# Attention kernel over 200 gathered histories: two of four row tiles fetched by address return to the gathers, scaling and copying move from TensorE to ScalarE, and every gather states its bound

## The chip, the cores and the metric

The kernel runs on one core of a Trainium2 chip. The metric is the device time of one execution in microseconds. TensorE is PE in the profile, VectorE DVE, ScalarE ACT, GpSimd POOL and SyncE SP.

## The reference

A recommendation model scores 16,384 samples. Each has a user, an item, a category and 200 history items. For every history position l the rows of an embedding table (100,000 rows of 64 floats) are gathered, a small attention layer gives each sample a weight, and the weighted rows are summed:

```
h = i_emb[hist]                               # [200, 16384, 64]
feat = concat([h, it, h - it, h * it])
a = dice(feat @ au_W1 + au_b1, au_alpha, axis=1)   # moments over the 16384 samples
cur = sum(((a @ au_W2) + au_b2) * h, axis=0)
z = concat([u, it, c, cur])
z = dice(z @ W1 + b1, alpha1, axis=0)
z = dice(z @ W2 + b2, alpha2, axis=0)
return z @ W3 + b3
```

`dice(x)` is `x * (p + alpha * (1 - p))` with `p = sigmoid((x - mean) * rsqrt(var + eps))`. History indices lie from 0 to 99,999, category indices below 1000.

## The kernel before

The 16,384 samples are 128 tiles of 128. Eight columns c of 16 tiles each make up one history position l, so the work is 200 x 8 = 1,600 steps k = 8l + c. A step has a row buffer `rows` of 128 x 16 x 64 (one of five, `ROWS`), and the steps overlap: in step k the rows of k are fetched, those of k-1 are transposed and multiplied (`turn`, `product`), those of k-2 are read out of PSUM and measured (`hidden`, `measure`), and those of k-10 (`LAG`) are weighted and added to the sum (`gate`, `weights`, `weigh`). After eight columns `moments` makes mean and variance of the position. The order on each engine is written out by hand in `step` (L368 to L392). Forty-five positions make up one pass of a loop (`LPB`); the loop runs four passes and the last 20 positions stand after it.

**Three ways bring rows in.** The usual one is `gather` (L124 to L130): one indirect transfer on POOL reads 128 indices from a column of `idx` and fetches 128 rows. It states no bound. Of the 128 tiles of a position 124 go this way (`NC`, L74), 16 in an even column and 15 in an odd one. The last tile of columns 1 and 5 goes through SP (`rows_by_sync`): SP loads addresses into registers 16 at a time and issues one transfer per row, 32 rows in each step (`ask`, L398). The last tile of columns 3 and 7 goes through ScalarE (`rows_by_scalar`): eight addresses at a time, 32 rows in each step at two places in its order (L379, L384), with three semaphores `landed` of its own and a wait ahead of the use (`await_rows_by_scalar`). `turn` copies such a tile, on ScalarE, from `side` or `aside` into the row buffer (L339).

**Two works stand on TensorE rather than on ScalarE.** `ph` is a copy of the transposed rows `hT` in PSUM, made by a product with the unit matrix (L341). The weight of a sample is `alpha * x + (1 - alpha) * p * x`, summed over the hidden units with `au_W2`; it is made as two products into `wb`, one of `xs` with `blk_x` and one of `y = pg * xs` with `blk_p` (L316).

The whole begins with 128 gathers of the items, and ends with 256 gathers of categories and users and the head (the two dense layers and the output).

Of the kernel before, what the change touches and what calls it, by code (L numbers as in the profile page):

```python
# [9 lines left out]
I32 = mybir.dt.int32  # L10
AF = mybir.ActivationFunctionType
ALU = mybir.AluOpType
PSUM = bass.MemoryType.PSUM

P = 128
D = 64
EPS = 1e-8
CH = 512
S = 32
# [3 lines left out]
LAG = 10  # L23
XR = 9
IDX = 3
BY_SP = (1, 5)
BY_ACT = (3, 7)
SIDES = (1, 3, 5, 7)
LOAD = 16
GROUP = 8  # L30
ROW = 4 * D
U8 = mybir.dt.uint8

# [2 lines left out]
def din_kernel(  # L36
# [32 lines left out]
    ZA = P // 2  # L69
    ZB = Z1 - ZA  # L70
    NS = len(SIDES)
    NB, NA = len(BY_SP), len(BY_ACT)
    serial = iter(range(10**6))
    NC = NT - NS  # L74
    BODY = L - L % LPB if L > LPB else 0
    STATS = nc.vector.BN_STATS_DIM
# [5 lines left out]
    def make(name, *shape, dt=F32):  # L82
        return const.tile(list(shape), dt, name=name)
# [4 lines left out]
    def quarter(e, g, n=S):  # L88
        return slice((2 * e + g) * S, (2 * e + g) * S + n)
# [23 lines left out]
    idx = [make(f"idx{i}", P, NC, dt=I32) for i in range(IDX)]  # L113
    ids = [make(f"ids{i}", P, NT, dt=I32) for i in range(3)]
    side = [make(f"side{i}", P, D) for i in range(3)]
    aside = [make(f"aside{i}", P, D) for i in range(3)]
    landed = [tc.alloc_semaphore(f"landed{i}") for i in range(3)]
    addrs = make("addrs", 2 * S + 1, NS * P, dt=I32)
    addr = [addrs[i * S : i * S + 1] for i in range(3)]
    stats = [make(f"st{i}", P, 2 * ND, STATS) for i in range(3)]  # L120
    rstds = [make(f"rs{i}", P, 1) for i in range(3)]
    shifts = [make(f"sh{i}", P, 1) for i in range(3)]
# [1 line left out]
    def gather(dst, ids, n, table):  # L124
        nc.gpsimd.indirect_dma_start(  # L125
            out=dst[:, n, :],
            out_offset=None,
            in_=table,
            in_offset=bass.IndirectOffsetOnAxis(ap=ids, axis=0),
        )  # L130

    def load_ids(t, v):
# [23 lines left out]
    def layer(dst, pairs, first=True, last=True):  # L156
        for i in range(2):
            for j, (lhsT, rhs) in enumerate(pairs):
                nc.tensor.matmul(  # L159
                    dst[:, ts(i, CH)], lhsT, rhs[:, ts(i, CH)],  # L160
                    start=(first and j == 0), stop=(last and j == len(pairs) - 1),
                    skip_group_check=not (first and last),
                )
# [9 lines left out]
    blk_h = make("blk_h", P, P)  # L173
    blk_i = make("blk_i", P, P)
    blk_m = make("blk_m", P, P)
    blk_p = make("blk_p", P, P)
    blk_x = make("blk_x", P, P)
    unit = make("unit", P, P)
    au_w = make("au_w", P, 4, A)
    au_bias = make("au_bias", P, 1)  # L180
    au_al = make("au_al", P, 1)
# [4 lines left out]

    def attention_weights():
        nc.vector.memset(eps, EPS)
        for t in (blk_h, blk_i, blk_m, blk_p, au_bias, au_al, au_w2):
            nc.vector.memset(t, 0.0)  # L190
        nc.sync.dma_start(au_bias2, au_b2.partition_broadcast(P))
        for e in range(2):
            w = au_W1.rearrange("(g d) a -> d g a", d=D)[e * S : (e + 1) * S]
            for g in range(2):
                r = quarter(e, g)
                nc.sync.dma_start(au_w[r], w)
                for q, (a0, n) in enumerate(halves):
                    c, a = quarter(q, g, n), slice(a0, a0 + n)
                    nc.vector.tensor_add(blk_h[r, c], au_w[r, 0, a], au_w[r, 2, a])
                    nc.vector.tensor_sub(blk_i[r, c], au_w[r, 1, a], au_w[r, 2, a])  # L200
                    nc.vector.tensor_copy(blk_m[r, c], au_w[r, 3, a])
                    nc.vector.memset(blk_p[r, quarter(q, g)], 1.0)
        for g in range(2):
            for q, (a0, n) in enumerate(halves):
                r, a = quarter(q, g, n), slice(a0, a0 + n)
                nc.sync.dma_start(au_bias[r], col(au_b1)[a])
                nc.sync.dma_start(au_al[r], col(au_alpha)[a])
                nc.sync.dma_start(au_w2[r], au_W2[a])
        nc.vector.tensor_scalar(au_1al, au_al, -1.0, 1.0, ALU.mult, ALU.add)
        nc.vector.tensor_mul(au_1al, au_1al, au_w2)  # L210
        nc.vector.tensor_mul(au_al, au_al, au_w2)
        nc.vector.tensor_scalar_mul(blk_x, blk_p, au_al)
        nc.vector.tensor_scalar_mul(blk_p, blk_p, au_1al)
        nc.vector.tensor_copy(unit, lanes)
        nc.vector.tensor_single_scalar(unit, unit, float(P), ALU.is_equal)


    w1a = make("w1a", P, 4, P)
# [10 lines left out]
    al1a, al1b, al12 = make("al1a", P, 1), make("al1b", P, 1), make("al12", P, 1)  # L229
    same_a = make("same_a", P, P)  # L230
    same_b = make("same_b", P, P)
    lanes, lane = (ucT[i][:, :P].bitcast(I32) for i in range(2))

    def head_weights():
        for t in (w1a, w1b, w2a, w2b, w3, bias2, al2):
# [28 lines left out]

    flat = i_emb.rearrange("v d -> (v d)").bitcast(U8)

    def addresses(l, s, p0, n, engine):
        _, at = nc.values_load_multi_w_load_instructions(
            addr[l % 3][:, s * P + p0 : s * P + p0 + n],
            engines=(engine,), min_val=0, max_val=ROW * (V - 1),  # L270
            skip_runtime_bounds_check_because="the DMA checks the address against the table",
        )
        return [flat[ds(a, ROW)].rearrange("(o d) -> o d", o=1) for a in at]

    def rows_by_sync(m, part, n):
        l, j = divmod(m, NB)
        s, dst = SIDES.index(BY_SP[j]), side[m % 3].bitcast(U8)
        for p0 in range(part * n, part * n + n, LOAD):
            for j, row in enumerate(addresses(l, s, p0, LOAD, mybir.EngineType.SP)):
                nc.sync.dma_start(dst[p0 + j : p0 + j + 1], row)  # L280


    keys = {}

    def rows_by_scalar(m, part):
        l, j = divmod(m, NA)
        s, dst = SIDES.index(BY_ACT[j]), aside[m % 3].bitcast(U8)
        key = keys.setdefault(m, f"rows{next(serial)}")
        for j, row in enumerate(addresses(l, s, part * GROUP, GROUP, mybir.EngineType.Activation)):
            p = part * GROUP + j  # L290
            dma = nc.scalar.dma_start(dst[p : p + 1], row).then_inc(landed[m % 3], 16)  # L291
            tc.no_tile_sem_insts.add(dma.ins.name)
            tc.add_to_no_dep_group(key, dma.ins)

    def await_rows_by_scalar(m):
        if m in keys:
            fence = nc.scalar.wait_ge(landed[m % 3], 16 * P)
            tc.declare_fence(fence.ins, group=keys.pop(m))
            nc.scalar.sem_clear(landed[m % 3])

    def has_side(k):
        return k % ND in SIDES
# [7 lines left out]
    def gate(k):  # L310
        i = k // ND % 3
        nc.scalar.activation(pg, xs[k % XR], AF.Sigmoid, bias=shifts[i], scale=rstds[i])  # L312

    def weights(k):
        nc.vector.tensor_mul(y, pg, xs[k % XR])  # L315
        layer(wb, [(blk_x, xs[k % XR]), (blk_p, y)])  # L316

    def weigh(k):
        nc.vector.scalar_tensor_tensor(wb, wb, au_bias2, hT[k % LAG], ALU.add, ALU.mult)  # L319
# [10 lines left out]
    def turn(k):  # L330
        if has_side(k):
            l, c = divmod(k, ND)
            if c in BY_ACT:
                m = l * NA + BY_ACT.index(c)
                await_rows_by_scalar(m)
                of = aside[m % 3]
            else:
                of = side[(l * NB + BY_SP.index(c)) % 3]
            nc.scalar.copy(rows[k % ROWS][:, TD - 1], of)  # L339
        transpose(hT[k % LAG], rows[k % ROWS])  # L340
        layer(ph, [(unit, hT[k % LAG])])  # L341
        layer(px, [(blk_h, hT[k % LAG]), (blk_i, itT[k % ND])], last=False)

    def product(k):
        nc.vector.tensor_mul(hm, ph, itT[k % ND])  # L345
# [22 lines left out]
    def step(k, last=None):  # L368

        def has(j):  # L370
            return last is None or j <= last

        if has(k):
            fetch(k)
        if has(k - LAG):
            gate(k - LAG)
            weights(k - LAG)
        if has(k):
            scalar_rows(k, 0)  # L379
        if has(k - 2):  # L380
            hidden(k - 2)
            measure(k - 2)
        if has(k):
            scalar_rows(k, 1)  # L384
        if has(k - 1):
            turn(k - 1)
        if has(k - LAG):
            weigh(k - LAG)
        if has(k - 1):
            product(k - 1)  # L390
        if has(k - 2) and (k - 2) % ND == ND - 1:
            moments((k - 2) // ND)  # L392

    AHEAD = ND // NB - 1 - BY_SP[0]

    def ask(k, end):  # L398
        m, part = divmod(k + 1 + AHEAD, ND // NB)
        if m < end * NB:  # L400
            rows_by_sync(m, part, P * NB // ND)

    def scalar_rows(k, slot):
        m, part = divmod(k, ND // NA)
        n = P * NA // ND // GROUP
        for i in range(n)[slot::2]:
            rows_by_scalar(m, part * n + i)

    def steps(l0, n, end):
        for k in range(n * ND):  # L410
# [10 lines left out]
    with tc.manual_schedule():  # L421
# [4 lines left out]
        load_ids(ids[2], r_user)  # L426
        nc.gpsimd.iota(lanes, pattern=[[1, P]], base=P, channel_multiplier=-1)
        attention_weights()
        for t in (*hT, *xs, *side, *aside, hm):
            nc.vector.memset(t, 0.0)  # L430
        for t in curT:
            nc.vector.memset(t, 0.0)
# [14 lines left out]
            if c:  # L447
                transpose(itT[c - 1], rows[(c - 1) % ROWS])
        nc.vector.memset(rows[-1 % ROWS], 0.0)
        for k in range(-1 - AHEAD, 0):  # L450
            ask(k, L)
        head_weights()

    if BODY:
        with tc.For_i(0, BODY, LPB) as l0:  # L455
            with tc.manual_schedule():
                steps(l0, LPB, LPB + 1)
                await_rows_by_scalar(LPB * NA - 1)

    K = (L - BODY) * ND  # L460
    za = [hT[(K - LAG + c) % LAG] for c in range(ND)]
# [140 lines left out]
```

## Time and profile before

| | us |
|---|---|
| median of three runs (31616.96 to 31647.4) | 31644.94 |
| the profiled execution | 31616.96 |
| its span, first instruction to last | 31615.1 |
| first gather of the history starts at | 162.8 |
| first gather of the head starts at | 31159.5 |
| last gather of the head starts at | 31477.8 |
| median of a gather on POOL | 0.944 |
| median from a gather's issue to landing | 2.4 |

The profile is of one execution. A group's row names line, engine, operation, output and inputs, count, then busy time and the mean of one in ns, then the idle time of the engine just before these instructions and what ended most of it. "Issue" means that the engine waited for nothing that the profile shows. A row of the timeline has start, duration, engine, line, operation and, in brackets, the idle time before it and its releaser. A row of waits has the waiting engine and line, the releaser, the total in us, the number of waits and the longest. A row with three durations separated by slashes has minimum, median and maximum in ns.

### The profile page before, as it was taken

The page shows a single profiled execution, that of the slowest core. Times are in us where ns is not written, and L with a number is a line of the kernel's source. Part 1 is how long each engine was busy: PE and PEld are TensorE (multiplying, and loading weights), DVE is VectorE, ACT ScalarE, POOL GpSimd, SP SyncE. Part 2 cuts the span into 40 slices and gives each one's busy share as a digit, 9 for nine tenths or more (in the row PEclk, how much of TensorE's full clock was granted, in tenths as well). Part 3 has the DMA queues.
Part 4 walks back from the last instruction along what each step waited for, and adds up shares of the span by engine and source line. Part 5 has one row for each costly group of instructions (what it writes and reads, how often), then busy time and mean ns, then how long its engine had stood idle before and what let it go on. Part 6 is the DMA issues. An engine that isn't in the chain of part 4 may idle for free. (4 is left out here: it accounts for less than half of the span.)

```text
span 31615.1 us, 357535 instructions
## 1 busy us (share of the span) xinstructions
PE 20448.2 (65%) x38864; PEld 8357.2 (26%) x38864; DVE 15015.4 (47%) x18963; ACT 4479.6 (14%) x4670; POOL 23766.1 (75%) x25189
## 2 busy tenths in 40 slices
PE   5666666666666666666666666666666666666666
PEld 2222222222222222222222222222222222222222
DVE  4444444444444444444444444444444444444443
ACT  1111111111111111111111111111111111111111
POOL 7777777777777777777777777777777777777776
PEclk7888888888888888888888888888888888888887
DMA  1111111111111111111111111111111111111111
GB/s 29 28 28 28 28 28 28 28 28 28 28 28 28 28 28 28 28 28 28 28 28 28 28 28 28 28 28 28 28 28 28 28 28 28 28 28 28 28 28 23
DMA packets 1050292, 890.26 MB, mean 28 GB/s; under 512 B 644640, under 2 KB 644640, under 8 KB 1047784
## 3 DMA queue, kind: packets, MB, share of 16 engines
q0 software_dynamic: 805888, 826.84, 11.8%
q1 hardware_dynamic: 138920, 27.05, 0.4%
q10 hardware_dynamic: 102976, 13.32, 0.3%
q14 instruction: 2202, 18.04, 0.2%
q8 instruction: 306, 5.01, 0.1%
HBM read 865.03 MB, written 0.13 MB: 27 GB/s over the span
## 5 line engine op out<-in xcount | busy, mean ns | idle before, releaser
L125 POOL DMA_INDIRECT rows<-in_L_rec_i_emb,idx x24800 | 23403.2, 944 | 7593.5 <-issue 7032.1
L159 PE MATMUL ph<-hT,unit 128*128 128x512 f32 x6404 | 5658.4, 1029 | 10498.9 <-DVE hT L154 10498.9
L154 DVE STREAM_TRANSPOSE hT<-rows 64x512 f32<-64x512 f32 x6404 | 4518.8, 706 | 8256.8 <-DMA rows<-in_L_rec_i_emb,idx 4150.3
L328 DVE BATCH_NORM_STATS2 st<-xs 128x6 f32<-128x512 f32 x3204 | 2060.4, 685 | 7172.9 <-ACT xs L323 7172.9
L159 PEld LDWEIGHTS ph<-hT,unit 128*128 128x128 f32 x6404 | 1688.5, 295 | 13506.4 <-DVE hT L154 13334.4
L159 PE MATMUL px<-hT,blk_h 128*128 128x512 f32 x6404 | 3936.6, 702 | 0.0
L323 ACT ACTIVATE xs<-px,au_bias 128x1024 f32<-128x1024 f32 x1602 | 1784.3, 1114 | 14626.1 <-PE px L159 12323.9
L159 PE MATMUL wb<-y,blk_p 128*128 128x512 f32 x6440 | 3329.8, 599 | 455.3 <-DVE y L315 455.3
L159 PE MATMUL px<-itT,blk_i 128*128 128x512 f32 x6404 | 3368.8, 608 | 0.0
L159 PE MATMUL wb<-xs,blk_x 128*128 128x512 f32 x6440 | 3307.3, 595 | 51.5 <-PEq L455 39.9
L159 PE MATMUL px<-hm,blk_m 128*128 128x512 f32 x6408 | 3013.0, 592 | 40.5 <-DVE hm L430 40.5
L312 ACT ACTIVATE pg<-xs,sh,rs 128x1024 f32<-128x1024 f32 x1610 | 1939.8, 1205 | 3751.2 <-issue 2579.9
L315 DVE TENSOR_TENSOR y<-pg,xs 128x1024 f32<-128x1024 f32 x1610 | 1956.6, 1215 | 512.9 <-ACT pg L312 508.6
L159 PEld LDWEIGHTS px<-hT,blk_h 128*128 128x128 f32 x6404 | 1566.7, 245 | 2295.1 <-issue 2294.6
L319 DVE SCALAR_TENSOR_TENSOR wb<-wb,au_bias,hT 128x1024 f32<-128x1024 f32 x1610 | 2080.5, 1292 | 88.2 <-PE wb L159 36.0
L320 DVE TENSOR_TENSOR curT<-wb,curT 128x1024 f32<-128x1024 f32 x1610 | 1970.8, 1224 | 54.8
L345 DVE TENSOR_TENSOR hm<-ph,itT 128x1024 f32<-128x1024 f32 x1601 | 1941.2, 1212 | 0.0
L159 PEld LDWEIGHTS px<-itT,blk_i 128*128 128x128 f32 x6404 | 1374.9, 215 | 1925.3 <-issue 1925.3
L159 PEld LDWEIGHTS wb<-y,blk_p 128*128 128x128 f32 x6440 | 1212.0, 191 | 2081.7 <-issue 1445.9
L159 PEld LDWEIGHTS wb<-xs,blk_x 128*128 128x128 f32 x6440 | 1228.3, 191 | 1603.9 <-issue 1597.9
L159 PEld LDWEIGHTS px<-hm,blk_m 128*128 128x128 f32 x6408 | 1218.1, 190 | 1573.0 <-issue 1424.7
L339 ACT COPY rows<-aside 128x64 f32<-128x64 f32 x401 | 97.9, 244 | 2659.6 <-DMA aside<-in_L_rec_i_emb 2525.7
(155 smaller groups left out, 2171.5 us busy)
## 6 DMA issues: line engine op xcount, KB each, us to landing
aside<-in_L_rec_i_emb ACTq DMA_DIRECT2D x51200, 0.2 KB
side<-in_L_rec_i_emb SPq DMA_DIRECT2D x51200, 0.2 KB
rows<-in_L_rec_i_emb,idx POOLq DMA_INDIRECT x24800, 2.4
idx<-in_r_hist SPq DMA_DIRECT2D x200, 62.0 KB
addrs<-in_r_hist SPq DMA_DIRECT2D x200, 2.0 KB
rows<-in_L_rec_i_emb,ids POOLq DMA_INDIRECT x128, 2.4
rows<-in_L_rec_c_emb,ids POOLq DMA_INDIRECT x128, 2.4
rows<-in_L_rec_u_emb,ids POOLq DMA_INDIRECT x128, 2.4
```

What stands on the lines that cost most here:

```text
L125: nc.gpsimd.indirect_dma_start(out=dst[:, n, :], out_offset=None, in_=table, in_offset=bass.IndirectOffsetOnAxis(ap=ids, axis=0),)
L154: nc.vector.transpose(by_tile(dst[ts(e, D)], i), of[ts(i, D), :, ts(e, S)])
L159: nc.tensor.matmul(dst[:, ts(i, CH)], lhsT, rhs[:, ts(i, CH)], start=(first and j == 0), stop=(last and j == len(pairs) - 1), skip_group_c ...
L312: nc.scalar.activation(pg, xs[k % XR], AF.Sigmoid, bias=shifts[i], scale=rstds[i])
L315: nc.vector.tensor_mul(y, pg, xs[k % XR])
L319: nc.vector.scalar_tensor_tensor(wb, wb, au_bias2, hT[k % LAG], ALU.add, ALU.mult)
L320: nc.vector.tensor_add(curT[k % ND], wb, curT[k % ND])
L323: nc.scalar.activation(xs[k % XR], px, AF.Identity, bias=au_bias)
L328: nc.vector.bn_stats(stats[l % 3][:, 2 * c + i, :], xs[k % XR][:, ts(i, CH)])
L339: nc.scalar.copy(rows[k % ROWS][:, TD - 1], of)
L345: nc.vector.tensor_mul(hm, ph, itT[k % ND])
```

## The change

Of the four tiles fetched by address two remain, both through SP: the last tiles of columns 3 and 7 (`SIDES = (3, 7)`). `NC` becomes 126. ScalarE issues no rows any more, and its semaphores and `aside` go. ScalarE does two works that TensorE did: it copies `hT` into `ph`, and it applies `au_al` and `au_1al` to `pg` in a second pass, so that one product with `blk_w` (the 0 and 1 blocks) is left of the two into `wb`. Every gather gets `bounds_check`, the last row of its table, and `oob_is_err=False`: an index beyond it is skipped, and no error is reported. In the built program this gives each gather a register operand for the bound and a register move in front of it on POOL.

```diff
-BY_SP = (1, 5)
-BY_ACT = (3, 7)
-SIDES = (1, 3, 5, 7)
+SIDES = (3, 7)
...
             in_offset=bass.IndirectOffsetOnAxis(ap=ids, axis=0),
+            bounds_check=table.shape[0] - 1,
+            oob_is_err=False,
         )
...
-    def rows_by_scalar(m, part):
-        l, j = divmod(m, NA)
-        s, dst = SIDES.index(BY_ACT[j]), aside[m % 3].bitcast(U8)
-        key = keys.setdefault(m, f"rows{next(serial)}")
-        for j, row in enumerate(addresses(l, s, part * GROUP, GROUP, mybir.EngineType.Activation)):
-            p = part * GROUP + j
-            dma = nc.scalar.dma_start(dst[p : p + 1], row).then_inc(landed[m % 3], 16)
...
+    def rows_by_address(m, l, part, n):
+        s, dst = m % NS, side[m % 3].bitcast(U8)
+        for b in range(0, n, LOAD):
+            p0 = part * n + b
+            _, at = nc.values_load_multi_w_load_instructions(
+                addr[l % 3][:, s * P + p0 : s * P + p0 + LOAD],
+                engines=(mybir.EngineType.SP,), min_val=0, max_val=ROW * (V - 1),
+                skip_runtime_bounds_check_because="the DMA checks the address against the table",
+            )
+            for j, a in enumerate(at):
+                p = p0 + j
+                nc.sync.dma_start(dst[p : p + 1], flat[ds(a, ROW)].rearrange("(o d) -> o d", o=1))
...
         nc.scalar.activation(pg, xs[k % XR], AF.Sigmoid, bias=shifts[i], scale=rstds[i])
+        nc.scalar.activation(pg, pg, AF.Identity, bias=au_al, scale=au_1al)
...
         nc.vector.tensor_mul(y, pg, xs[k % XR])
-        layer(wb, [(blk_x, xs[k % XR]), (blk_p, y)])
+        layer(wb, [(blk_w, y)])
...
         transpose(hT[k % LAG], rows[k % ROWS])
-        layer(ph, [(unit, hT[k % LAG])])
         layer(px, [(blk_h, hT[k % LAG]), (blk_i, itT[k % ND])], last=False)
+        nc.scalar.copy(ph, hT[k % LAG])
...
-        if has(k):
-            scalar_rows(k, 0)
...
-        if has(k):
-            scalar_rows(k, 1)
...
-    AHEAD = ND // NB - 1 - BY_SP[0]
+    PER = ND // NS
 
     def ask(k, end):
-        m, part = divmod(k + 1 + AHEAD, ND // NB)
-        if m < end * NB:
-            rows_by_sync(m, part, P * NB // ND)
+        m, part = divmod(k + 1, PER)
+        if m < end * NS:
+            rows_by_address(m, m // NS, part, P // PER)
```

## The prediction

> **What bounds the kernel now.** I read the busy times first, then the groups, then POOL's own timeline, then who waits for whom.
>
> ```profile
> PE 20448.2 (65%) x38864; PEld 8357.2 (26%) x38864; DVE 15015.4 (47%) x18963; ACT 4479.6 (14%) x4670; POOL 23766.1 (75%) x25189
> POOL 7777777777777777777777777777777777777776
> ```
>
> POOL is the busiest at 75%, evenly over all slices; a share of 75% alone does not say that it is the bound. The group of its gathers does:
>
> ```profile
> L125 POOL DMA_INDIRECT rows<-in_L_rec_i_emb,idx x24800 | 23403.2, 944 | 7593.5 <-issue 7032.1
> ```
>
> Busy and idle together, 23403.2 + 7593.5 = 30,996.7 us, are nearly the span, and nearly all idle time is "issue": it waits for nothing. The timeline of POOL in mid-run and at a loop edge:
>
> ```profile
> 15000.58 0.94 POOL L125 DMA_INDIRECT rows<-in_L_rec_i_emb,idx  x1 [0.30 <-issue]
> 15001.83 0.94 POOL L125 DMA_INDIRECT rows<-in_L_rec_i_emb,idx  x1 [0.30 <-issue]
> 15003.08 0.94 POOL L125 DMA_INDIRECT rows<-in_L_rec_i_emb,idx  x1 [0.30 <-issue]
> ...
> 7129.46 0.94 POOL L125 DMA_INDIRECT rows<-in_L_rec_i_emb,idx  x1 [0.30 <-issue]
> 7139.70 0.94 POOL L125 DMA_INDIRECT rows<-in_L_rec_i_emb,idx  x1 [9.30 <-issue]
> ```
>
> A gather starts every 1.25 us: 0.94 of work and a fixed 0.30 between two. The only breaks are four loop edges with idle times of 9.30, 7.51, 7.51 and 2.96 us, 26.1 us over the usual 0.30. So the pitch is (30,996.7 - 26.1) / 24,800 = **1.2488 us**. Everyone else waits for it:
>
> ```profile
> PEld ph L159 <- DVE hT L154: 13334.4, 3201, 17.2
> ...
> DVE hT L154 <- DMA rows<-in_L_rec_i_emb,idx: 4150.3, 753, 7.8
> DVE hT L154 <- ACT rows L339: 3143.2, 579, 6.5
> ```
>
> TensorE waits for the transposes, and these for gathered rows (or for ScalarE's copy of a tile fetched by address). The kernel's time is a count of gathers times a pitch.
>
> **The change part by part.**
>
> *Two tiles go back to POOL.* NC goes from 124 to 126 gathers per l. Over 200 l that is 400 more, with no cover, on the engine that sets the end: 400 x 1.2488 = **+499.5 us**. The 128 gathers of the items and 256 of the head stay, so the changed kernel has 25,200 + 384 = 25,584.
>
> *ScalarE's address work goes.* Its 51,200 transfers, register moves and waits leave (16 rows took 6.27 us in the timeline, so 51,200 some 20,000 us of its queue), and with them q10's 0.3% of the DMA engines. None of this holds a gather back, so it gives nothing. What is late next is what was late before: the gather.
>
> *SP's rows keep their count and lead.* It issued columns 1 and 5 and now issues 3 and 7, again 51,200. A tile's last part is asked two steps before its copy in both (before: step 8l for step 8l+2; after: 8l+2 for 8l+4). A step becomes 15.75 gathers, 19.7 us, against 19.4. Nothing.
>
> *TensorE gives work to ScalarE.* The `unit` products into `ph` (5658.4 us) and the `blk_x` half of the weights (3307.3 us) go. ScalarE gets a 128x1024 copy into `ph` per step, like the L323 row (1114 ns), and a second pass over `pg`, like L312 (1205 ns). Per step it then has 1.2 + 1.2 + 1.1 + 1.1 us and copies and table loads, about 5.2 of 19.7. The copy waits for the transposes, and behind it in the queue stands the next step's gate; `y` on VectorE waits for that. The chain from landing on (copy 0.24, transposes 2.9, `ph` 1.1, `hm` 1.2, two products 1.9, `xs` 1.1) is 8.4 us, gate, second pass and `y` 3.6 more: within a step, and the five row buffers give more. Costed at nothing; the cover is 19.7 us of gathers, and a chain past that would cost its excess 1,600 times.
>
> *The register move.* In the built program every gather gets a register move (the bound) in front of it on POOL's queue, 25,584 of them. SP's row shows one:
>
> ```profile
> L280 SPq MOVE side<-in_L_rec_i_emb x51200: 29/29/38, 52.6 to 31022.5; - x200
> ```
>
> With the gap after it, it delays SP's next issue by 59 ns. On POOL there is cover: I set the records of its 537 semaphore waits in the first loop pass against their place in the program. 393 ran 7 gathers ahead of the running one, 104 ran 6 and 37 ran 8 ahead, and a gather during which one ran has the same median pitch, 1249 ns. The queue is far ahead of the worker, so 59 ns vanish; without that cover they cost 25,584 x 0.059 = 1,509 us.
>
> *The check itself* is what no row shows: the worker compares 128 indices with a bound and would leave some out (none here: the drawn indices are all inside the tables). The nearest rows on POOL are:
>
> ```profile
> L588 POOL MEMSET const-uint8-127<- 128x1 uint8 x1 | 0.1, 116 | 0.0
> L588 POOL MEMSET const-float32-0.0<- 128x1 f32 x1 | 0.1, 99 | 0.3 <-issue 0.3
> ```
>
> One instruction over one value per partition, the shape of an index column, takes 99 to 116 ns with everything around it. Upper end: a whole pass, +0.116 x 25,584 = +2,968 us. A gain is not excluded, since the error path goes; but with no index out of range that can save little more than a scalar step, nearest the 29 ns move. Lower end: -0.029 x 25,584 = -742 us. I take **zero**, the row it is nearest to being the gather itself, 128 rows in 944 ns whatever the table (i_emb, c_emb and u_emb all 944): a compare in a loop that already reads, scales and writes out each index should vanish.
>
> A rule speaks against the change. The gather spends 944 / 128 = 7.4 ns per row. The Trainium skill's "GPSIMD Engine Reference", section 3.1, says that data-dependent branching costs about 12 cycles an element on these cores, whose clock section 1 gives as 1.2 GHz. If the skip were such a branch it would cost, as an estimate from that page, 10 ns x 128 = 1.28 us a gather, and the sum would be near 64.9 ms. The row shows a loop cheaper per row than one such branch; no run here shows the skip yet.
>
> **The sum.** Span 31,615.1 + 499.5 = 32,114.6; the profiled execution took 31,616.96, 1.9 more: 32,116.5. That execution was the lowest of three, whose median is 31,644.94; from the median it is 32,144.4. I take 32,130, +1.5%.
>
> **Rivals.**
>
> *A, forecast: the bound is free.* 32,130, own range 31,900 to 32,400 (a pitch of -8 to +10 ns). For: the wait records, and the equal 944. Chance 0.45.
>
> *B, the check costs worker time.* Halfway to the upper end, 0.058 x 25,584 = +1,484, about 33,600; at the end 35,085. For: the gather of before carries no bound at all in the built program, so work is added, and every nanosecond of it is paid 25,584 times. Against: the 0.30 us between gathers could take in a little. Chance 0.28.
>
> *C, the other side: leaving out the error report shortens the gather.* It decides from the point where the two extra gathers are paid: 499.5 / 25,584 = 19.5 ns a gather. At 29 ns: 32,116 - 742 = 31,374, faster by 0.8%. For: no other engine needs more than SP's 32 rows at 0.39 us, 12.5 of a step's 19.7 us, so every nanosecond would count. Against: nothing is reported in either kernel. Chance 0.19.
>
> *D, the register operand ends the run-ahead.* Were each move held until the gather before it had read its register, 59 ns show: 32,116 + 1,509 = 33,625. For: the operand is read from a register that the next move writes again. Against: the waits, which also stand between gathers, held nothing back. Chance 0.06.
>
> *E, no bound reaches the worker.* Against: the built program has the register as an operand of every gather. The time is A's. Chance 0.02.
>
> **How the numbers follow.** About 0.2% is what a measurement can tell from no change, a pitch window of 5 ns here: it takes 0.03 from C and B together. Faster 0.18, within 0.2% 0.03, slower 0.79. The range runs from C's price to B's end, 31,370 to 35,085; beyond lie the deeper half of C and a per-index branch, some 0.16.
>
> **What would show it.** Right: 25,200 body gathers at 944 ns with 0.30 between; POOL idle on issue; ScalarE near 8.2 ms busy, TensorE near 11.5 ms. B: the mean of L117's group above 944 with the gap unchanged. D: gap near 0.36 with 944 unchanged. C: the mean below 925. Wrong altogether: POOL idle on a releaser other than issue for more than a few hundred us, above all on VectorE through the row buffers (ScalarE's copy into `ph` too late).

## The result, and the profile after

The changed kernel took **33,488 us** (median of four runs, 33,485.28 to 33,488.41) against 31,645.5 before: a ratio of 1.058, with a 95% interval of 1.057 to 1.060. The forecast was 32,130, and the rival that came true is B, the check that costs worker time (about 33,600). The profiled execution has a span of 33,486.4, 1,871.3 more than that of before.

POOL's busy share is nearly the same (76% against 75%), and so is its idle time for each gather. The busy times and the gathers' group:

```profile
PE 15624.0 (47%) x26020; PEld 6240.6 (19%) x26020; DVE 14943.1 (45%) x18956; ACT 7826.6 (23%) x7481; POOL 25517.3 (76%) x25589
...
L117 POOL DMA_INDIRECT rows<-in_L_rec_i_emb,idx x25200 | 25133.8, 997 | 7713.3 <-issue 7139.6
```

The count is 25,200, as forecast, but the mean of one is 997 ns where it was 944. Idle before is 7713.3 / 25,200 = 306 ns, as before. In the timeline the starts are 1.30 us apart instead of 1.25, and all of the difference is in the busy part:

```profile
15001.07 1.00 POOL L117 DMA_INDIRECT rows<-in_L_rec_i_emb,idx  x1 [0.30 <-issue]
15002.38 1.00 POOL L117 DMA_INDIRECT rows<-in_L_rec_i_emb,idx  x1 [0.31 <-issue]
15003.68 1.00 POOL L117 DMA_INDIRECT rows<-in_L_rec_i_emb,idx  x1 [0.30 <-issue]
```

Nobody else became the bound. In the list of waits POOL waits for "issue", and VectorE for gathered rows, now three times as long as before. The 3,143.2 us in which it waited for ScalarE's copy of fetched tiles have no row any more:

```profile
DVE hT L148 <- DMA rows<-in_L_rec_i_emb,idx: 12714.8, 1498, 10.2
POOL rows L117 <- issue: 7250.3, 23693, 8.1
```

The register moves are in the trace, on POOL's queue, one for each gather:

```profile
L117 POOLq MOVE  x25584: 29/29/39, 0.8 to 33339.7; - x200
```

They ran seven or eight gathers ahead of the running one in 25,194 of 25,584 cases. During 22,067 of the 25,584 gathers no move ran, and these took 997.4 ns in the mean, the other 3,517 took 997.2, so the moves are hidden. The sum in measured terms: 400 gathers x 1.2488 = 499.5 us, and 25,584 x (997.4 - 943.7) ns = 1,374 us, together 1,873 of the 1,871 measured.

In the runs of experiments 1 to 12 many instructions on SP's queue, and on ScalarE's where it issues rows, took 700 ns where the profile of before has 29 and 228 on SP's, and the kernel before took 49,000 us on these chips, so that of those runs only the gathers' durations are read; the cause was not found, and on one of the same chips it was gone later.

### The profile page after: what moved, and what is told of

It is laid out like the page before. It is cut to its first block, busy times and chain, and to the rows that moved or that the text cites. A ratio compares the mean times of both kernels' runs of the same rounds, so it can differ in the third digit from the quotient of the medians.

```text
span 33486.4 us, 250048 instructions
## 1 busy us (share of the span) xinstructions
PE 15624.0 (47%) x26020; PEld 6240.6 (19%) x26020; DVE 14943.1 (45%) x18956; ACT 7826.6 (23%) x7481; POOL 25517.3 (76%) x25589
## 3 DMA queue, kind: packets, MB, share of 16 engines
q0 software_dynamic: 818688, 839.97, 11.3%
## 5 line engine op out<-in xcount | busy, mean ns | idle before, releaser
L117 POOL DMA_INDIRECT rows<-in_L_rec_i_emb,idx x25200 | 25133.8, 997 | 7713.3 <-issue 7139.6
L153 PE MATMUL px<-hT,blk_h 128*128 128x512 f32 x6404 | 5631.5, 978 | 16412.0 <-DVE hT L148 16412.0
L306 ACT COPY ph<-hT 128x1024 f32<-128x1024 f32 x1601 | 1627.7, 1017 | 20119.3 <-DVE hT L148 20119.3
L153 PEld LDWEIGHTS px<-hT,blk_h 128*128 128x128 f32 x6404 | 1816.1, 314 | 19421.0 <-issue 18597.0
L153 PE MATMUL px<-itT,blk_i 128*128 128x512 f32 x6404 | 4715.2, 829 | 0.0
L153 PE MATMUL wb<-y,blk_w 128*128 128x512 f32 x6440 | 3417.2, 657 | 1285.9 <-DVE y L284 1270.4
L153 PEld LDWEIGHTS px<-itT,blk_i 128*128 128x128 f32 x6404 | 1851.6, 289 | 2836.5 <-issue 2836.5
L281 ACT ACTIVATE pg<-pg,au_al,au_1al 128x1024 f32<-128x1024 f32 x1610 | 1896.1, 1178 | 54.0
L153 PEld LDWEIGHTS wb<-y,blk_w 128*128 128x128 f32 x6440 | 1309.1, 207 | 3019.1 <-issue 1542.3
```

What stands on the lines that cost most here:

```text
L117: nc.gpsimd.indirect_dma_start(out=dst[:, n, :], out_offset=None, in_=table, in_offset=bass.IndirectOffsetOnAxis(ap=ids, axis=0), bounds_c ...
L153: nc.tensor.matmul(dst[:, ts(i, CH)], lhsT, rhs[:, ts(i, CH)], start=(first and j == 0), stop=(last and j == len(pairs) - 1), skip_group_c ...
L281: nc.scalar.activation(pg, pg, AF.Identity, bias=au_al, scale=au_1al)
L306: nc.scalar.copy(ph, hT[k % LAG])
```

## The experiments

The theory: stating a bound makes POOL's worker compare the indices, which takes some 53 ns of every gather and reaches the time in full. The rivals: that skipping takes the time and not the comparison (2); that ScalarE's new work or the two tiles do (3); that the register move does (4).

### 1, 5, 11 and 13: the change without its bound

```diff
             in_offset=bass.IndirectOffsetOnAxis(ap=ids, axis=0),
-            bounds_check=table.shape[0] - 1,
-            oob_is_err=False,
         )
```

This kernel was run four times; its time is read from the last run.

> The changed kernel without the two arguments of the gather; all else as changed (two tiles by address, ScalarE's copy and second pass). Theory 1 (the bound check takes time in POOL's worker, 53 ns a gather): gathers back at 944 ns, pitch 1.249 us, span 31,615 + 400 x 1.2488 = 32,115 us, time 32,115 to 32,145. Theory 2 (the skip mode, not the comparison, takes it): the same here. Rival 3 (the bound is free, and the gather is slowed by ScalarE's new work, the lower clock of TensorE or the 126-column index tile): gathers stay at 997 ns, time 33,490.

> The kernel of the first experiment once more, since the transfers by address of SP and ScalarE, not the gathers, set the time of all four runs of that call (register moves of 700 ns on both queues, where the profile of before has 29). Theory 1 (a stated bound costs 50 to 70 ns a gather, nothing else in the change does): where SP's moves take 29 ns, 944 ns a gather and 32,115 to 32,145 us. Rival 3 (ScalarE's new work or the two tiles cost more than their 400 gathers): 944 ns a gather, but a time above 32,200. Where the moves take 700 ns, again a time of some 47,000 that tells nothing of this.

> The kernel of the first experiment, for a chip on which SP's register moves take 29 ns as in the profile of before. Theory 1: 32,115 to 32,145 us. Rival 3 (ScalarE's new work or the two tiles cost more than their 400 gathers): above 32,200. Where the moves take 700 ns again: some 47,000.

> The changed kernel without the bound. Where the kernel before takes 31,620 us: by theory 1 32,115 to 32,145 us, 944 ns a gather. By rival 3 (ScalarE's copy and second pass delay the row buffers) above 32,200, with POOL waiting for transposes.

Measured: gathers of 943.9, 946.3, 946.3 and 945.5 ns, so that runs of one kernel differ by up to 2.4 ns. In the last run the time was 32,156 us against 31,674 of the kernel before on that chip, a ratio of 1.0152 (1.0135 to 1.0169). POOL's group there:

```profile
L117 POOL DMA_INDIRECT rows<-in_L_rec_i_emb,idx x25200 | 23825.5, 945 | 7709.1 <-issue 7267.6 <-DMA rows<-in_L_rec_i_emb,idx 417.0 <-DMA side<-in_L_rec_i_emb 21.4
```

So without the bound the change costs 482 us, where the 400 gathers alone were put at 499.5. Rival 3 falls: ScalarE's copy and second pass, the lower clock of TensorE and the wider index tile cost nothing. This is the forecast's case A, and its 1.5% was right for it.

### 2 and 14: the kernel before with the bound added

```diff
             in_offset=bass.IndirectOffsetOnAxis(ap=ids, axis=0),
+            bounds_check=table.shape[0] - 1,
+            oob_is_err=False,
         )
```

> The kernel before with the two arguments added to its gather and nothing else. Theories 1 and 2: gathers at 997 ns, 31,615 + 25,184 x 0.0535 = 32,962 us of span, time 32,960 to 32,990. Rival 3: gathers at 944 ns, time 31,645.

> The kernel before with the bound added. By theory 1 31,615 + 25,184 x 0.0535 = 32,962 us, 997 ns a gather. Rival: the rows by address hide some of it, less than 32,900.

Measured: gathers of 996.1 and 998.5 ns; in the second run 32,998.5 us against 31,674, a ratio of 1.0418 (1.0401 to 1.0435), so +1,324 us, or 1,324 / 25,184 = 52.6 ns a gather:

```profile
L125 POOL DMA_INDIRECT rows<-in_L_rec_i_emb,idx x24800 | 24761.9, 998 | 7593.8 <-issue 6964.2 <-DMA rows<-in_L_rec_i_emb,idx 617.7 <-ACT xs L325 5.5
```

The two lines alone make the old kernel 4.2% slower, and idle time stays where it was (7,593.8 against 7,593.5): nothing of the bound is hidden.

### 3 and 15: the bound with the error report

```diff
             bounds_check=table.shape[0] - 1,
-            oob_is_err=False,
         )
```

> The changed kernel with the bound stated, but an index beyond it reported as an error rather than skipped. Theory 1 (the comparison with the bound costs): 997 ns, time 33,490. Theory 2 (skipping costs): 944 ns, 32,115 to 32,145. A value between shares the 53 ns out between the two.

> The changed kernel with the bound and the error report. A gather took 1,012 ns in the earlier run, 15 more than with the skip; by theory 1 that is 25,584 x 0.015 = 380 us over the changed kernel, 33,870 us. Rival (the error report is free and the earlier 15 ns were that chip's): 33,490.

Measured: 1,011.7 ns a gather in both, and 33,848 us in the second, a ratio of 1.0686 (1.0669 to 1.0704) to the kernel before on its chip:

```profile
L117 POOL DMA_INDIRECT rows<-in_L_rec_i_emb,idx x25200 | 25494.9, 1012 | 7706.1 <-issue 7162.0 <-DMA rows<-in_L_rec_i_emb,idx 534.1 <-DMA side<-in_L_rec_i_emb 6.7
```

Rival 2 falls: with errors instead of skips a gather is not shorter but 14 ns longer. Beside what both forms have there is thus a smaller piece that the error form has and the skip form has not.

### 4: errors off, no bound stated

```diff
             in_offset=bass.IndirectOffsetOnAxis(ap=ids, axis=0),
-            bounds_check=table.shape[0] - 1,
             oob_is_err=False,
         )
```

> The changed kernel without the stated bound, but with errors switched off. No register operand and no move. Theory 1: 944 ns, time 32,115 to 32,145. Theory 2: 997 ns, time 33,490. If leaving out the error report saves something by itself, below 944 ns.

Measured: 946.3 ns a gather, within the 943.9 to 946.3 that the form with errors had on these chips. Where no bound is stated, leaving out the error report saves nothing; the forecast's case C had its gain from there.

### 12: a register move alone

```diff
+        nc.gpsimd.to_reg(table.shape[0] - 1)
         nc.gpsimd.indirect_dma_start(
...
-            bounds_check=table.shape[0] - 1,
-            oob_is_err=False,
```

> The changed kernel without the two arguments, but with a register move of its own ahead of every gather on POOL's queue, whose register no gather reads. Theory 1: the move is hidden (the queue is some eight gathers ahead) and a gather stays at 944 ns with 305 ns behind it: the 53 ns belong to the worker's comparison. Theory 4 (the move or its place in the queue costs): 997 ns, or a gap of 0.36 us. Time where SP's moves take 29 ns: 32,115 to 32,145 by theory 1, 33,490 to 33,620 by theory 4; otherwise some 47,000 either way.

Measured: 943.9 ns, and a median gap of 305 ns. But the moves are not in the run. Its trace has none on L117 or L118, and it has as many instructions as the kernel of experiment 1 (first and second line), 25,584 fewer than the changed kernel (third line):

```profile
span 46565.2 us, 224464 instructions
span 47013.0 us, 224464 instructions
span 33486.4 us, 250048 instructions
```

In effect this run repeats experiment 1 and says nothing of rival 4. The trace of the changed kernel does: the gathers during which no move ran took 997.4 ns, as long as the others, and the gap behind a gather has a median of 305 ns with and without the bound. A move's time on the queue is thus not what lengthens a gather. Whether the gather's reading of the register is a part of the 53 ns was not tested.

### 6: half of the rows skipped

```diff
-            bounds_check=table.shape[0] - 1,
+            bounds_check=table.shape[0] // 2 - 1,
...
-        for t in (*hT, *xs, *side, hm):
+        for t in (*rows, *hT, *xs, *side, hm):
```

> The changed kernel with the bound at half of each table (49,999 of 100,000 rows, and half of the categories), so that about half of the rows of every gather are skipped; they keep what their buffer had, and the buffers are zeroed at the start. Theory 1a (the comparison is made for each index without a branch, and a skipped row still gets a descriptor): 997 ns as in the changed kernel. Theory 1b (a skipped row is left out of the list, each by a branch): the mean moves away from 997 ns, down by up to 64 x 7.4 = 470 ns if a row left out saves its share of the 944 ns, up if the branch costs more than the row.

```profile
L117 POOL DMA_INDIRECT rows<-in_L_rec_i_emb,idx x25200 | 25148.2, 998 | 21026.9 <-DVE hT L148 12994.5 <-issue 7610.9 <-DMA rows<-in_L_rec_i_emb,idx 183.7
```

Measured: 998.0 ns a gather. A skipped row costs POOL what a fetched one costs, so no cost of a branch per skipped index shows. That rows were skipped shows in POOL's DMA queue, which moved 427.21 MB, where the kernel without the bound moved 839.97 on the same chip (experiment 5). Both have 818,688 packets, 32 for each gather, so a skipped row saves bytes and no packets.

### 7 and 8: gathers of 64 rows, with and without the bound

```diff
-            out=dst[:, n, :],
+            out=dst[:64, n, :],
...
-            in_offset=bass.IndirectOffsetOnAxis(ap=ids, axis=0),
+            in_offset=bass.IndirectOffsetOnAxis(ap=ids[:64], axis=0),
```

> The changed kernel, but every gather fetches 64 rows instead of 128 (partitions 64 to 127 of the row buffers stay zero), bound stated. Beside the same without a bound. If the bound is compared row by row, it adds 53.5 / 2 = 27 ns here; if it is a fixed step of the instruction, 53 ns again. The whole gather: 997 / 2 = 500 ns if all of it goes by rows, 720 if half of it is fixed.

> Gathers of 64 rows as in the kernel beside it, without the bound. All by rows: 944 / 2 = 472 ns. The difference to the kernel beside it is the price of the bound for 64 rows: 27 ns if it goes by rows, 53 ns if it is fixed. The time may then be set by SP's rows (12.5 us a step), so only the durations count.

The second kernel also leaves out the bound. The groups of the two:

```profile
L117 POOL DMA_INDIRECT rows<-in_L_rec_i_emb,idx x25200 | 23720.7, 941 | 23386.4 <-DVE hT L148 15473.1 <-issue 7677.5 <-DMA rows<-in_L_rec_i_emb,idx 131.2
L117 POOL DMA_INDIRECT rows<-in_L_rec_i_emb,idx x25200 | 22758.2, 903 | 24311.4 <-DVE hT L146 16409.1 <-issue 7629.8 <-DMA rows<-in_L_rec_i_emb,idx 170.2
```

Measured: 941.3 and 903.1 ns. The gathers of 128 rows on the same chip took 998.0 ns with a bound (experiment 6, where half of the rows are skipped) and 946.3 without (experiment 5). This gives a table with two differences in it:

| ns a gather | 64 rows | 128 rows | per row |
|---|---|---|---|
| no bound | 903.1 | 946.3 | 0.68 |
| bound | 941.3 | 998.0 | 0.89 |
| the bound's price | 38.2 | 51.7 | 0.21 |

Both guesses on the gather as a whole (500 or 720 ns) fell: half the rows save 43 ns. Taken as straight lines through two points, the gather is 860 ns fixed and 0.68 ns a row, and the bound 25 ns fixed and 0.21 ns a row. The bound's price is neither a fixed step alone nor a matter of rows alone: the 13.5 ns between 38.2 and 51.7 are more than the 2.4 ns by which runs of one kernel differ. The part that grows with the rows fits a comparison of each index; which step takes the fixed 25 ns is not shown. A gather of 64 rows has 32 packets on POOL's DMA queue, like one of 128 (818,688 in all, with half the bytes), so the packets are a candidate for the fixed 860 ns, which no run tests.

### 9 and 10: no tile by address

> The changed kernel with no tile by address at all: 128 gathers for each l, bound stated. 25,600 + 384 = 25,984 gathers. Theory 1 (time = gathers times pitch, and the stated bound makes the pitch 0.997 + 0.305 = 1.302 us): 25,984 x 1.302 + some 165 us ahead and after = 34,000 us, on any chip, since SP and ScalarE issue no rows. If the chips of the last two calls hold every engine back, and not only SP's and ScalarE's rows: well above, some 47,000.

> The kernel beside it without the bound. Theory 1: 25,984 x 1.2488 + 165 = 32,610 us; the difference to the kernel beside it 25,984 x 0.0535 = 1,390 us, all of it the bound's. Rival 3 (the bound's 53 ns do not reach the time one for one): a smaller difference.

The edit sets `SIDES = ()`, so that all 128 tiles go through POOL, and drops what loads addresses. Measured: gathers of 998.6 and 943.9 ns, but times of 38,185 and 37,910 us, both off the expected 34,000 and 32,610: POOL waited 4,032 and 5,191 us for the transposes, with or without the bound. ScalarE stood idle for 18,011.5 and 17,415.7 us ahead of `xs` for a release that the profile calls remote, of which the profile of after has no row. The two runs were meant to show POOL alone and did not; the next three do.

### g1, g2 and g3: the gathers alone

```diff
         if has(k):
             fetch(k)
-        if has(k - LAG):
-            gate(k - LAG)
-            weights(k - LAG)
...
-            ask(k, end)
             step(k)
```

All other work of the steps goes, and the loads of addresses. The second kernel also drops the bound, the third drops it and has `SIDES = (1, 3, 5, 7)`.

> Of the changed kernel's steps only the gathers are left (126 for each l, bound stated); the rows by address, transposes, products and sums are left out, so the output is not the reference's. 25,584 gathers. Theory 1: 25,584 x (0.997 + 0.305) + some 165 us = 33,480 us. If the bound's 53 ns are partly hidden as soon as no other engine reads the rows: less, down to 32,110.

> The same without the bound: 25,584 x 1.2488 + 165 = 32,115 us by theory 1, 1,370 below the kernel beside it. Rival 3 (the bound is not what lengthens the time): no difference between the two.

> The same with 124 gathers for each l and no bound, the gathers of the kernel before: 25,184 x 1.2488 + 165 = 31,615 us by theory 1, 500 below the kernel with 126 and 1,870 below the one with 126 and the bound.

Measured: 33,435, 32,094.5 and 31,600.5 us; the whole kernel before took 31,618.7 on that chip, so the third has a ratio of 0.9994 (0.9985 to 1.0004) to it. The groups of the first two:

```profile
L117 POOL DMA_INDIRECT rows<-in_L_rec_i_emb,idx x25200 | 25097.5, 996 | 7698.2 <-issue 7677.4 <-PEq L384 14.2 <-DMA rows<-in_L_rec_i_emb,idx 3.7
```

```profile
L117 POOL DMA_INDIRECT rows<-in_L_rec_i_emb,idx x25200 | 23774.5, 943 | 7701.8 <-issue 7681.2 <-PEq L382 14.1 <-DMA rows<-in_L_rec_i_emb,idx 3.7
```

The first less the second, 1,340 us, is the bound; the second less the third, 494 us, the 400 gathers; together 1,834.5, where the whole kernels differ by 1,842.5. All of the change's price is on POOL, and all other work of the kernel before takes 18 us beyond its gathers.

## Why the prediction was wrong, point by point

- *What bounds the kernel*: right. The gathers alone take 31,600 us, the whole kernel 31,619.
- *Two tiles go back to POOL*, +499.5 us: right; 494 us with the gathers alone, 482 in the whole kernel.
- *ScalarE's address work, SP's rows*: costed at nothing, and nothing came of them.
- *TensorE gives work to ScalarE*: the time was right, nothing. ScalarE's busy time became 7.8 ms (8.2 forecast). TensorE's became 15.6 ms and not 11.5, since some of its remaining products grew longer (those of `hT` from 702 to 978 ns) at a lower granted clock, 0.711 on average against 0.81 before; POOL covered that.
- *The register move*: right; hidden, seven or eight gathers ahead. Rival D fell with it: the gap stayed at 0.305 us.
- *The check itself*, "I take **zero** ... a compare in a loop that already reads, scales and writes out each index should vanish": **this step failed.** The term was put at nothing; it is 53 ns a gather, +1,374 us of the 1,871. No row showed such a loop: the equal 944 ns for three tables say nothing of how the time goes by rows, and the 7.4 ns a row (944 / 128) took all of it to go by rows. By the gathers of 64 rows it is 0.7 ns a row and, on a straight line through two points, 860 ns that do not go by rows. Work added to the gather had nothing to hide behind, since the gap of 305 ns stayed as it was; the register move was free, as it runs on the queue, ahead of the worker.
- *The bounds of the unknown* held: 53 ns lies between -29 and +116. Case B was priced halfway to the upper one, at 0.058 us and 33,600 us, and came out at 33,488; that the half came so near is luck, as the prediction gives no reason for it. Its reason for B was right: added work is paid 25,584 times.
- *Case C*: the error report saves 14 ns only once a bound is stated; against the kernel before, which states none, there was nothing to save.
- *The rule on branches* (the Trainium skill, "GPSIMD Engine Reference", section 3.1, 12 cycles an element) does not describe this check: with half of the rows skipped a gather took 998.0 ns, and the bound adds 53 ns and not the 1.28 us that the prediction estimated from the page.

## What to carry to other kernels

On an engine whose worker sets the time, an argument that looks free is priced as an instruction of its own until a run shows otherwise, and here it is paid 25,584 times. Before a cost is said to vanish inside a loop, measure the loop at two sizes: a mean divided by its count hides the fixed part. In this kernel queue work ahead of the busy worker was free, and work inside the worker was not; the two want separate lines in a sum. And before a run is read as a test, count in its trace that what was added is there: experiment 12 shows why.

## What the runs showed of the hardware

- A gather's time on POOL depends little on its rows: 903.1 ns for 64 and 946.3 for 128, with 305 ns to the next in both.
- TensorE's mean granted clock fell from 0.81 to 0.711 when its share fell from 65% to 47%, and products of the same shape grew from 608 to 829 ns (px from itT), while those of px from hm, later in the step, stayed at 592 and 596. The Trainium skill's "TensorE: Matmul & The Clock Gate", part 1, says that the gate is throttled by default and that activity releases it, which agrees with these two numbers; the gathers alone, with TensorE at 1%, showed 0.503 in 10 executions and 0.996 in 8, which it does not explain.
